# Where the gated cross-attention mixes a batch, when it asks for the transposed scores, and which step holds which projection product

## The chip, the core and the metric

The kernel runs on one core of a Trainium2 chip. The core has a matrix engine (PE, with its own weight loads, PEld), a vector engine (DVE), a scalar engine (ACT), a general engine (POOL) and a sequencer that issues DMAs (SP); 16 DMA engines serve the core. Each engine works through its own list of instructions in order and waits on semaphores for the others. The metric is the device time of one execution in microseconds (us), here the median of several.

## The reference, cut to what matters

Sixteen batches of 128 tokens with 512 features pass through a decoder layer (self-attention, cross-attention to `ctx_2048`, an MLP) and then through a gated cross-attention. All three attentions have 16 heads of 32 features. All is float32. The part that the change touches is the attention itself:

```
def attention(q, k, v, mask):
    scores = jnp.einsum('bhqd,bhkd->bhqk', q, k) / jnp.sqrt(jnp.float32(HD))
    scores = scores * mask - 10000.0 * (1.0 - mask)
    probs = jax.nn.softmax(scores, axis=-1)
    return jnp.einsum('bhqk,bhkd->bhqd', probs, v)
...
Q = (hidden_states @ Wq.T)...
K = (a @ Wk.T)...
V = (a @ Wv.T)...
attn = jax.nn.softmax(scores, axis=-1)
out = jnp.einsum('bhts,bhsd->bhtd', attn, V)
return hidden_states + jnp.tanh(gate) * out
```

The first function is the decoder's (used twice), the lines after the dots are the gated attention's.

## The kernel before

**Stages.** The program has three stages. The decoder's two attentions come first, then the MLP, then the gated attention. Tile names end in the attention's letter: A is self-attention, B the decoder's cross-attention, D the gated attention. The sixteen batches are worked in four groups ("sections") of four; the decoder has eight sections (A0 to A3, then B0 to B3), the gated attention four (D0 to D3).

**Units and steps.** `attend` (called once for the decoder with `ready` false, once for the gated attention with `ready` true) runs over steps numbered `k`. A batch takes four steps and its scores (`sc`, four banks of PSUM) are made on PE at the step with `k % 4 == 0`. A unit is four heads of one batch; each step adds one unit. Unit `u` is masked and its least value found on DVE around step `u` (`scale_unit`; the list `SCALED` puts the first unit of a batch in its first step, the second and third in the next, the fourth in the one after), exponentiated on ACT at step `u + 1` (`exp_unit`), normalised on DVE (a reciprocal) and POOL at `u + 2` (`norm_unit`), and turned on DVE and sent to DRAM (`away`) by SP at `u + 3` (`turn_unit`). Two units are fetched back in another order as one pair into a `pT` tile by four DMAs on SP (`receive_pair`). `pT` has three buffers and the `s` tile of a unit seven. The last four units of the gated attention are turned on PE instead (`turn_by_array`, `tp`).

**Mixing.** `mix` multiplies the weights of one batch, its two pairs, with the values `v` on PE (`av`). ACT then copies the result out (`mT`). Two steps later the result is projected by PE (`mo`), or, in the first three gated groups, put away for a later projection. The dictionaries `mixed_at` and `received_at` (line 702 on) hold in which step batch `b` is mixed and in which two steps its pairs are asked for. In a decoder step that makes scores the mixing stands at the head of the step, before the scores; the gated run mixes later in the step, after the step's jobs, and copies out at the start of the next step.

**What else a step does.** In the order of the code: asking for pairs, the work left over from the step before (`due`: DVE sums first, then ACT copies), the step's jobs, the projection of an earlier batch, the preparation of a later section (`prepare`: loads, transposes, copies into `T` tiles by ACT), turning, exponentials and normalisation, masking. While one section's attention runs, the jobs make the next section's queries, keys and values. Each of these three is a product cut into seven quarter-size products (Strassen's scheme, `block_product`), eight matmuls of 256 columns each, numbered 1 to 7. Products 1, 6 and 7 share the bank `mm0` and are copied out by ACT; 5 and 3 share `mm1`, 2 and 4 take `pt` banks, and DVE adds these up. The sums of inputs that the products need come from POOL. `GATED_BLOCKS` (line 508) says which of the 16 steps of a section holds which of the seven products of queries, keys and values. While the last section D3 runs, the output projections of the first three groups take their place (`deferred_jobs`).

**Order.** The engines keep the program's order (`InOrder`), so the step and the place in it fix the order on each engine and in SP's queue. Nearly every instruction goes through the recording helper at line 51, so the profile's rows all carry L51 and are told apart by tile.

```
SCALED = ((0,), (1, 2), (3,), ())
...
if ready and b * GB == last:
    k = last + 7
else:
    for half in range(2):
        received_at.setdefault(at + 2 * half, []).append(b * GB + 2 * half + 1)
mixed_at[k] = b
...
beside_scores = done is not None and m == 0
```

With `GB` = 4, unit number `b * GB + 1` stands for the first pair of batch `b`, `b * GB + 3` for the second. `last` is the first unit of the last batch.

Of the kernel before, what the change touches and what calls it, by code (L numbers as in the profile page):

```python
# [26 lines left out]
GB = 4  # L27
# [27 lines left out]
def decoder_then_gated_cross_attention(ctx: ExitStack, tc: tile.TileContext, a: dict, out: bass.AP):  # L55
# [24 lines left out]
    def afterwards(engine, do):  # L80
        late[engine].append(do)

    def due():

        left = [do for queue in (late["dve"], late["act"]) for do in queue]
        for queue in late.values():
            queue.clear()
        for do in left:
            do()
# [396 lines left out]
    def by_quarters(t):  # L486
# [20 lines left out]
    FIRST_CROSS_BLOCKS = {6: (1,), 7: (2, 6), 8: (5,), 9: (7, 4), 11: (3,)}, CROSS_BLOCKS[1]  # L507
    GATED_BLOCKS = (
        {0: (1,), 1: (2, 6), 2: (5, 7), 3: (4,), 5: (3,)},
        {5: (1,), 6: (2, 6), 7: (7,), 8: (5,), 9: (4,), 10: (3,)},  # L510
        {11: (1, 2), 12: (6,), 13: (5, 7), 14: (4,), 15: (3,)},
    )
    DEFERRED_BLOCKS = (
        {0: (1,), 1: (2, 6), 2: (5, 7), 3: (4,), 5: (3,)},
# [31 lines left out]
    def scores(bt):  # L546
        sec, t = bt.sec, slice(bt.b * S, (bt.b + 1) * S)
        for j in range(GB):
            bt.sc[j] = ps("sc", f"sc_{bt.name}_{j}")
        for c in range(KC):  # L550
            for j in range(GB):
                r = slice(j * HD, (j + 1) * HD)
                nc.tensor.matmul(
                    bt.sc[j][:, c * S : (c + 1) * S], sec.q[r, c, t], sec.k[r, c, t], start=True, stop=True
                )
# [4 lines left out]
    def by_head(t):  # L560
        return t.rearrange("p n c j -> p c n j")
# [59 lines left out]
    def receive_pair(bt, j):  # L621

        pT = work.tile([P, NQ, 2, KC, Q], F32, tag="pT", name=f"pT_{bt.name}_{j}", bufs=3)
        for m in range(NQ):
            nc.sync.dma_start(
                out=pT[m * Q : (m + 1) * Q].rearrange("k n u c q -> k n (u c q)"),
                in_=bt.away[j // 2][m].rearrange("(n k) u x -> k n (u x)", k=Q),
            )
        for u in range(2):
            bt.pT[j - 1 + u] = pT[:, :, u]  # L630

    def mix(bt):
        sec, b = bt.sec, bt.b
        av = ps(mixed_in[0], f"av_{bt.name}")
        for c in range(KC):
            for j in range(GB):
                h = c * GB + j
                nc.tensor.matmul(
                    av[j * HD : (j + 1) * HD, c * S : (c + 1) * S], sec.v[:, b, h * HD : (h + 1) * HD],
                    bt.pT[j][:, :, c, :], start=True, stop=True,  # L640
                )
        at_end = work.tile([P, KC, S], F32, tag="s", name=f"mT_{bt.name}", bufs=7) if bt.by_array else None
        mT = bt.mT = sec.mixed_tile(b) if at_end is None else at_end

        def mixed_out():
            if sec.v_bias is None:
                nc.scalar.copy(mT, av.rearrange("p (c q) -> p c q", q=S))
            else:
                for c in range(KC):
                    nc.scalar.activation(  # L650
                        mT[:, c], av[:, c * S : (c + 1) * S], AF.Identity, bias=col(sec.v_bias[0], sec.v_bias[1] + c)
                    )

        return mixed_out

    def out_project_last(bt):

        for n in range(2):
            at_ = slice(n * HF, (n + 1) * HF)
            mm = ps("mm", f"mo_{bt.name}_{n}")  # L660
            for c in range(KC):
                nc.tensor.matmul(
                    mm[:, 0:HF], bt.mT[:, c, :], bt.sec.w_o[:, c, at_], start=(c == 0), stop=(c == KC - 1)
                )
            bt.sec.finish(mm[:, 0:HF], bt.b, at_)

    def out_project(bt):
        mm = ps(mixed_in[0], f"mo_{bt.name}")
        for c in range(KC):
            nc.tensor.matmul(mm, bt.mT[:, c, :], bt.sec.w_o[:, c, :], start=(c == 0), stop=(c == KC - 1))  # L670
        afterwards("dve", lambda: bt.sec.finish(mm, bt.b))
# [13 lines left out]
    def attend(sections, ready, others, after=None):  # L685

        if not ready:
            sections[0].start(sections[1])
        units, batches = [], []
        projected = deque()

        last = (len(sections) * GB - 1) * GB

        def by_transfer(n):

            return min(n, last) if ready else n  # L700

        mixed_at, received_at = {}, {}
        for b in range(len(sections) * GB):
            k, at = (b + 3) * GB, (b + 2) * GB
            sooner = 2 if ready else min(2, max(0, b + 4 - len(sections) * GB))
            k, at = k - sooner, at - sooner
            if ready and b * GB == last:
                k = last + 7
            else:
# [4 lines that stand above are left out]
        def step(k, bt=None, jobs=(), ahead=None):  # L714

            m = k % GB
            mixed_in[0] = "sc" if not ready and k > last + 2 else "mm"
            pairs, done = received_at.get(k, []), mixed_at.get(k)
            beside_scores = done is not None and m == 0
            if beside_scores:  # L720
                mixed_out = mix(batches[done])
            if m == 0 and bt is not None:
                scores(bt)
            for pair in pairs:
                receive_pair(*units[pair])
            due()
            if beside_scores:
                mixed_out()
                projected.append((k, batches[done]))
            for job in jobs:  # L730
                job()
            last_mix = ready and k == last + 7
            if last_mix:
                afterwards("act", mix(batches[-1]))
                projected.append((k, batches[-1]))
            if projected and k - projected[0][0] >= (1 if ready and bt is None else 2):
                before = projected.popleft()[1]
                if before.by_array:
                    out_project_last(before)
                elif before.sec.deferred:  # L740
                    afterwards("act", lambda: before.sec.put_away(before))
                else:
                    out_project(before)
            first_turned = ready and k == last + 6
            if first_turned:
                turn_by_array(*units[k - 3])
            if done is not None and not (beside_scores or last_mix):
                mixed_out = mix(batches[done])
                if ready:
                    afterwards("act", mixed_out)  # L750
                else:
                    mixed_out()
                projected.append((k, batches[done]))
            if ahead is not None:
                ahead.prepare(k % NS)
            if 0 <= k - 3 < len(units) and not first_turned:
                (turn_unit if k - 3 < by_transfer(k) else turn_by_array)(*units[k - 3])
            def norm():
                if 0 <= k - 2 < len(units):
                    norm_unit(*units[k - 2])  # L760

            def exp():
                if 0 <= k - 1 < len(units):
                    least_unit(*units[k - 1])
                    exp_unit(*units[k - 1])


            for do in (exp, norm) if ready else (norm, exp):
                do()
            if bt is not None:  # L770
                for j in SCALED[m]:
                    scale_unit(bt, j)
                if bt.b < sec.by_head_from:
                    bt.sec.add_mask(by_head(bt.s[m]), bt.b)

        k = 0
        for i, sec in enumerate(sections):
            jobs = others() if i + 1 == len(sections) else sections[i + 1].jobs()
            ahead = sections[i + 2] if i + 2 < len(sections) else after if i + 2 == len(sections) else None
            for b in range(GB):  # L780
                bt = Batch(sec, b)
                batches.append(bt)
                for m in range(GB):
                    units.append((bt, m))
                    step(k, bt, jobs.get(k % NS, ()), ahead)
                    k += 1
        while projected or k < len(units) + 2 * GB:
            step(k, jobs=jobs.get(k - len(units) + NS, ()))
            k += 1
# [1038 lines left out]
```

## Time and profile before

| what | value |
|---|---|
| median of 3 runs | 1159.51 us (1159.28 to 1161.2) |
| the profiled execution's own time | 1162.35 us |
| its span, first to last instruction | 1160.6 us |
| PE busy in it | 1132.9 us |
| decoder, first to last mixing on PE | 84.3 to 553.2 us |
| gated attention, first scores to end | 946.1 to 1160.6 us |
| DMA traffic, mean over the span | 224 GB/s |

The profile comes from one execution with the hardware profiler on. Its span is what the views below are drawn on; the time of that same execution stands 1.75 us above its span, and 2.84 us above the median of the unprofiled runs. A row of the timeline gives the start, the duration, the engine, the tiles written and read and how many instructions were merged in it; in square brackets stands how long the engine had been idle and what ended the wait. SPq rows are DMAs being issued; the landing comes later. Matmul ends are modelled, so rows of PE overlap by about 0.1 us.

### The profile page before, as it was taken

What the parts mean: (1) busy time and instruction counts of PE and PEld (TensorE: products, weight loads), DVE (VectorE), ACT (ScalarE), POOL (GpSimd) and SP (SyncE); (2) the same over time, 40 slices, a digit from 0 to 9 for tenths busy, and PEclk for the clock granted to TensorE, in tenths of its full rate; (3) what the DMA queues carried; (4) which work ended last, traced back from release to release, by engine and by line L of the source; (5) the groups of instructions that cost most, each with busy time, mean ns of one, the idle gap of its engine ahead of it and who ended that gap; (6) DMA issues with size and microseconds to landing.
All of it is one profiled execution on the core that took longest, in us unless ns stands there. A gap on an engine that the chain in (4) does not pass through costs nothing.

```text
span 1160.6 us, 22182 instructions
## 1 busy us (share of the span) xinstructions
PE 1132.9 (98%) x7246; PEld 875.1 (75%) x7246; DVE 742.9 (64%) x1919; ACT 612.0 (53%) x2142; POOL 694.4 (60%) x633
## 2 busy tenths in 40 slices
PE   9999999999999999989899999999999999999998
PEld 8877777666666757446688888888888877878875
DVE  6678978798787786866554634443342247767754
ACT  3567676767767766663231233223222237867663
POOL 6798888788868675752333514443342168545883
PEclk9999999999999999989999999999999999999999
DMA  6688878999889889997787696697447827987975
GB/s 220 162 206 227 228 208 212 280 232 255 209 221 222 218 231 254 297 272 247 236 260 238 189 280 192 200 283 254 154 154 234 258 51 200 249 236 222 272 216 175
DMA packets 325285, 259.81 MB, mean 224 GB/s; under 512 B 83561, under 2 KB 280625, under 8 KB 320305
## 3 DMA queue, kind: packets, MB, share of 16 engines
q1 hardware_dynamic: 325128, 258.38, 78.1%
q8 instruction: 58, 0.95, 0.4%
q14 instruction: 59, 0.48, 0.1%
q10 hardware_dynamic: 40, 0.01, 0.0%
HBM read 163.94 MB, written 94.37 MB: 223 GB/s over the span
## 4 chain that ended last, share of the span: by engine, by line
PE 45%; DMA 6%; POOL 2%; DVE 2%; SPq 1%; ACT 1%; issue 1%; DVEq 0%; ACTq 0%; POOLq 0%
PE o L51 16%; PE h L51 15%; PE mm_v_D L51 4%; PE mm_q_D L51 3%; PE mm_o_D L51 1%; DMA back_x<-turned_x 1%; DMA pT_D<-away_D 1%; PE mm_k_D L51 1%; DMA pT_B<-away_B 1%; SPq L51 1%; PE av_D L51 1%; DMA away_D<-s_D 1%; PE mo_D L51 1%; DMA away_B<-s_B 1%; PE sc_D L51 1%
## 5 line engine op out<-in xcount | busy, mean ns | idle before, releaser
L51 DVE TENSOR_TENSOR h<-h,h 128x512 f32<-128x512 f32 x80 | 54.9, 686 | 113.9 <-PE h L51 113.9
L51 ACT ACTIVATE h<-h 128x512 f32<-128x512 f32 x64 | 40.3, 630 | 162.3 <-DVE h L51 162.3
L51 ACT ACTIVATE s_A<-s_A,mn_A 128x128 f32<-128x128 f32 x256 | 99.4, 391 | 45.7 <-issue 23.8
L51 ACT ACTIVATE s_B<-s_B,mn_B 128x128 f32<-128x128 f32 x256 | 99.4, 392 | 29.7 <-issue 14.0
L51 POOL TENSOR_TENSOR s_D<-s_D,sum_D 128x512 f32<-128x512 f32 x64 | 66.5, 1040 | 59.9 <-DVE sum_D L51 53.1
L51 POOL TENSOR_TENSOR s_B<-s_B,sum_B 128x512 f32<-128x512 f32 x64 | 66.8, 1044 | 56.4 <-DVE sum_B L51 47.8
L51 ACT ACTIVATE s_D<-s_D,mn_D 128x128 f32<-128x128 f32 x256 | 99.1, 392 | 0.4 <-issue 0.4
L51 POOL TENSOR_TENSOR s_A<-s_A,sum_A 128x512 f32<-128x512 f32 x64 | 66.5, 1039 | 31.0 <-DVE sum_A L51 25.3
L51 POOL TENSOR_TENSOR s_A<-s_A,ma 128x512 f32<-128x512 f32 x64 | 81.8, 1279 | 5.1 <-DVE s_A L51 4.1
L51 POOL TENSOR_TENSOR s_B<-s_B,mask 128x512 f32<-128x512 f32 x60 | 76.4, 1273 | 2.4 <-DVE s_B L51 1.5
L51 POOL TENSOR_TENSOR rstd_aD<-rstd_aD,mhalf 128x1 f32<-128x1 f32 x12 | 6.6, 549 | 114.8 <-DVE rstd_aD L51 101.6
L51 POOL TENSOR_TENSOR sh<-h 128x512 f32<-128x512 f32 x32 | 40.7, 1272 | 50.8 <-ACT h L51 49.9
L51 PE MATMUL h<-sx,t 128*128 128x256 f32 x256 | 60.6, 379 | 2.0 <-ACT h L51 2.0
L51 PE MATMUL h<-T_C,w 128*128 128x256 f32 x256 | 61.2, 382 | 1.3 <-DVE h L51 1.3
L51 PE MATMUL h<-T_C,t 128*128 128x256 f32 x256 | 60.6, 379 | 1.0 <-DVE h L51 1.0
L51 PE MATMUL o<-t,h 128*128 128x256 f32 x256 | 60.5, 379 | 0.0
L51 PE MATMUL o<-w,h 128*128 128x256 f32 x256 | 60.5, 379 | 0.0
L51 PE MATMUL o<-t,sh 128*128 128x256 f32 x256 | 60.5, 379 | 0.0
L51 DVE CUSTOM_DVE_ANT_0 s_D<-sc_D,gmask 128x128 f32<-128x128 f32 x256 | 57.1, 283 | 1.0 <-DMA turned_x<-x_D 0.9
L51 PE MATMUL mo_A<-w_ao,mT_A 128*128 128x512 f32 x128 | 57.5, 592 | 0.0
L51 PE MATMUL mo_B<-w_co,mT_B 128*128 128x512 f32 x128 | 57.5, 592 | 0.0
L51 PE MATMUL mm_q_B<-T_B,w_cq 128*128 128x512 f32 x128 | 57.4, 596 | 0.0
(335 smaller groups left out, 3007.4 us busy)
## 6 DMA issues: line engine op xcount, KB each, us to landing
t<-kept SPq DMA_DIRECT2D x24, 1024.0 KB, 8.3
away_A<-s_A SPq DMA_DIRECT2D x64, 256.0 KB, 3.3
pT_A<-away_A SPq DMA_DIRECT2D x128, 128.0 KB, 3.8
away_B<-s_B SPq DMA_DIRECT2D x64, 256.0 KB, 3.3
pT_B<-away_B SPq DMA_DIRECT2D x128, 128.0 KB, 4.8
away_D<-s_D SPq DMA_DIRECT2D x60, 256.0 KB, 3.4
pT_D<-away_D SPq DMA_DIRECT2D x120, 128.0 KB, 2.8
w<-in_L_xattn_w_dram SPq DMA_DIRECT2D x24, 512.0 KB, 5.5
```

Source lines behind the costliest of these rows:

```text
L51: return lambda *args, **kw: self.tc.keep_in_program_order(call(*args, **kw))
```

## The change

The change touches two places.

```
     GATED_BLOCKS = (
         {0: (1,), 1: (2, 6), 2: (5, 7), 3: (4,), 5: (3,)},
-        {5: (1,), 6: (2, 6), 7: (7,), 8: (5,), 9: (4,), 10: (3,)},
-        {11: (1, 2), 12: (6,), 13: (5, 7), 14: (4,), 15: (3,)},
+        {4: (1,), 5: (2,), 6: (6,), 7: (5, 7), 9: (4, 3)},
+        {9: (1,), 10: (2, 6), 11: (5,), 12: (7,), 13: (4,), 15: (3,)},
     )
...
         for b in range(len(sections) * GB):
-            k, at = (b + 3) * GB, (b + 2) * GB
-            sooner = 2 if ready else min(2, max(0, b + 4 - len(sections) * GB))
-            k, at = k - sooner, at - sooner
+            sooner = min(2, max(0, b + 4 - len(sections) * GB))
+            k, at = (b + 3) * GB - sooner, (b + 2) * GB - max(1, sooner)
```

In steps, for batch `b` (the last three batches of a run have their own numbers, by `sooner`):

| run | pairs asked for, before | after | mixed, before | after |
|---|---|---|---|---|
| decoder, batches 0 to 28 | 4b+8, 4b+10 | 4b+7, 4b+9 | 4b+12, head | 4b+12, head |
| decoder, batches 29 to 31 | unchanged | | unchanged | |
| gated, batches 0 to 12 | 4b+6, 4b+8 | 4b+7, 4b+9 | 4b+10, after the jobs | 4b+12, head |
| gated, batch 13 | 4b+6, 4b+8 | 4b+7, 4b+9 | 62 | 63, after the jobs |
| gated, batches 14, 15 | unchanged | | unchanged | |

So the gated run's mixing moves two steps later, to the head of a step with the next-but-two batch's scores, and its result is copied out by ACT within that step instead of at the start of the next one. The projection or putting away that follows two steps after a mixing moves with it. The products of the next section's keys and values move to the steps shown; the queries' stay. No instruction is added or taken away on any engine, and POOL's list is the same, instruction by instruction.

Between two scores of the gated run PE now finds these products of the next section (q, k, v with the number of the product), in the order of its list:

| steps of a section | before | after |
|---|---|---|
| 0 to 3 | q1 q2 q6 q5 q7, mixing, q4 | q1 q2 q6 q5 q7 q4, mixing |
| 4 to 7 | q3 k1 k2 k6, mixing, k7 | k1 q3 k2 k6 k5 k7, mixing |
| 8 to 11 | k5 k4 k3, mixing, v1 v2 | k4 k3 v1 v2 v6 v5, mixing |
| 12 to 15 | v6 v5 v7 v4, mixing, v3 | v7 v4 v3, mixing |

The mixing at the end of each "after" row is the one at the head of the following step, just ahead of its scores.

## The prediction

> **What bounds the kernel now.** I read the page's busy times first, then the list of waits of PE, then PE's timeline around the long waits, then the other engines there.
>
> ```profile
> PE 1132.9 (98%) x7246; PEld 875.1 (75%) x7246; DVE 742.9 (64%) x1919; ACT 612.0 (53%) x2142; POOL 694.4 (60%) x633
> ```
>
> PE is idle for 1160.6 - 1132.9 = 27.7 us. The change adds and removes no instruction, so it can win only from those 27.7 us and from what a lowered matrix clock costs inside the busy time. The waits say which part is in reach:
>
> ```profile
> PE av_B L51 <- DMA pT_B<-away_B: 6.7, 2, 5.5
> PE av_D L51 <- DMA pT_D<-away_D: 3.0, 3, 2.3
> ...
> PE sc_D L51 <- DVE mn_D L51: 0.9, 1, 0.9
> ...
> PE mm_k_D L51 <- ACT k_D L51: 0.7, 1, 0.7
> ```
>
> The columns are sum, count and longest. The first two rows are mixings (`av`) whose pair had not landed. The largest one, in section B3, is at step 124:
>
> ```profile
> 504.13 0.41 PE L51 MATMUL av_B<-pT_B,v_B 128*32 128x128 f32 x4
> 510.09 1.92 PE L51 MATMUL av_B<-pT_B,v_B 128*32 128x128 f32 x28 [5.54 <-DMA pT_B<-away_B]
> 511.94 2.09 PE L51 MATMUL sc_B<-k_B,q_B 32*128 32x128 f32 x32
> 513.96 4.71 PE L51 MATMUL mm_v_D<-w_gv,T_a 128*128 128x512 f32 x8
> 518.51 3.60 PE L51 MATMUL mo_B<-w_co,mT_B 128*128 128x512 f32 x8
> ```
>
> Four matmuls on the first pair run, the other 28 wait for the second. After the wait the same work is slower: 1.92 us where 28 such matmuls take 1.07 elsewhere, 2.09 where scores take 1.17, 4.71 where eight matmuls of 512 columns take 3.60. That is 0.85 + 0.92 + 1.11 = 2.9 us more, and the granted clock from 508 to 514 us is 0.60. So this wait costs 5.5 + 2.9 = 8.4 us. The gated attention has a smaller copy of it in D1, and the rows after it show a stretch that I need below:
>
> ```profile
> 1024.33 0.41 PE L51 MATMUL av_D<-pT_D,v_D 128*32 128x128 f32 x4
> 1027.05 1.07 PE L51 MATMUL av_D<-pT_D,v_D 128*32 128x128 f32 x28 [2.31 <-DMA pT_D<-away_D]
> 1028.05 5.38 PE L51 MATMUL mm_v_D<-w_gv,T_a 128*128 128x256 f32 x16
> 1033.36 1.17 PE L51 MATMUL sc_D<-k_D,q_D 32*128 32x128 f32 x32
> 1034.46 1.99 PE L51 MATMUL mm_v_D<-gsums,gsums_a 128*128 128x256 f32 x8
> 1036.29 1.89 PE L51 MATMUL mm_v_D<-w_gv,gsums_a 128*128 128x256 f32 x8
> 1038.02 1.89 PE L51 MATMUL mm_v_D<-gsums,T_a 128*128 128x256 f32 x8
> ...
> 1044.50 1.17 PE L51 MATMUL sc_D<-k_D,q_D 32*128 32x128 f32 x32
> ```
>
> Sixteen such matmuls take 3.72 us elsewhere, here 5.38: 1.7 us of clock (granted 0.72 from 1026 to 1032). This wait costs 2.3 + 1.7 = 4.0 us.
>
> **The change, part by part.** *Asking one step sooner in the decoder.* The late pair is asked for at step 122; it moves to the head of step 121, just behind the send of step 120.
>
> ```profile
> 498.33 0.38 SPq L51 DMA_DIRECT2D away_B<-s_B  x1
> 499.16 0.34 SPq L51 DMA_DIRECT2D kept_v_D<-v_D  x1
> ...
> 502.23 1.95 SPq L51 DMA_DIRECT2D pT_B<-away_B  x4
> ```
>
> Its four issues would start at 498.8 instead of 502.2, 3.4 us sooner. Its inputs are away since 491.3 and its buffer was freed by the mixing that ended at 496.0, so nothing holds it. What it is moved past on SP is one `kept_v_D` store, two `back_C` loads, one weight load and the send of unit 118. They start 2 us later. The loads feed the MLP, which starts at 526 us, the store the gated attention; the send's pair is asked for at 511.65. Now its landing:
>
> ```profile
> 503.88 6.12 DMA pT_B<-away_B
> ```
>
> This row of the chain of waits says that the last of the four, issued at 503.88, landed after 6.12 us. At the same price the new one lands at 510.0 - 3.4 = 506.6. PE is there at 504.5, so 2.1 us of the 5.5 stay: 3.4 gained. The other decoder wait, 1.1 us at 465, is shorter than a step and goes; if SP moves up with PE the gain there carries over whole, if not it lengthens the rest of the big wait. I take half, 0.6. For the clock I have 2.9 now, and afterwards a gap of 2.1 to 3.2 us, near the 2.31 that cost 1.7; gaps of 1.12, 1.73 and 1.96 us elsewhere left the clock at 1.00. Half of 1.7 gives a gain of 2.9 - 0.8 = 2.1. Sum 3.4 + 0.6 + 2.1 = 6.1. The next to be late would be the mixing at 525.5. Its pair stays where it is, issued from 511.65; with 1.65 between first and last issue and a median landing of 5.4 us (transfers into `pT_B`, 440 to 560 us) it is there at 518.7, and PE would come at 519.4. It just fits. Bounds: nothing (the pair lands when the busy DMA engines let it) and 6.7 + 2.9 = 9.6.
>
> The Trainium skill, page "DMA: Bandwidth & Descriptors", section on the anatomy of one DMA (on GpSimd's path), puts a transfer at about 2 us plus its bytes by 436 GB/s, which makes an estimated 2.3 us for 128 KB; the 6.12 us above were measured with the DMA engines busy throughout (share 1.06 from 508 to 514). By the page the pair would land at 502.8, the wait would vanish and the decoder would gain 9.6; the row decides.
>
> *Mixing two steps later, asked for one step later, in the gated run.* A pair gets three steps from its last send to the request instead of two, and three to its mixing. SP waited 42.9 us in 29 places for `away_D` to land before it could ask. I count all three `av_D` waits but the one at the end (0.4, on the unchanged batches) as gone: 0.32 + 2.31, and 1.7 of clock. Bounds 0 and 4.3; what hides the landing now is two steps of products.
>
> *Products in other steps.* k7 no longer follows k6 at once, so the 0.68 wait for ACT's copy in D0 goes; k5 now stands ahead of the scores that waited 0.92 there, so these meet finished masks. Gain 1.6, bounds 0 and 1.6. But the 21 products of a section, 6+5+5+5 between the scores, become 6+6+6+3. In the last quarter PE has two products less to do while DVE still needs the same chain: the last mask of a batch stands behind the reciprocal of its first unit, that behind the unit's exponentials, those behind ACT's copies. In D1:
>
> ```profile
> 1036.49 0.59 ACT L51 COPY v_D<-mm_v_D 128x512 f32<-128x512 f32 x1 [2.63 <-PE mm_v_D L51]
> 1036.97 0.82 ACT L51 ACTIVATE T_a<-back_a,vcols 128x512 f32<-128x512 f32 x1
> ...
> 1039.94 0.59 ACT L51 COPY v_D<-mm_v_D 128x512 f32<-128x512 f32 x1 [0.62 <-PE mm_v_D L51]
> 1040.43 0.82 ACT L51 ACTIVATE T_a<-back_a,vcols 128x512 f32<-128x512 f32 x1
> ```
>
> The first copy is of v6, the second of v7, and the chain ends with the last mask at 1043.86. After the change v7 has v6's place and the second copy is gone: ACT is free at 1039.24 and saves 1.2 us to 1040.43. The mask ends at 1042.7. PE saves v6 and v5, 1038.02 - 1034.46 = 3.6, and wants to start the scores at 1044.50 - 3.56 = 1040.9. A new wait of 1.7 us at `sc_D`. The same reading of D0 (mask ends at 993.23, ACT saves 1.2, scores at 993.26 - 3.56) gives 2.3; in D2, where DVE is held by POOL's normalisation, 1089.45 - 1.05 against 1090.80 - 3.56 gives 1.1. D3 keeps its products. Sum 5.1, and half of 1.7 for the clock after the 2.3 us gap: 5.9. Queued behind are only PE's next products; they wait with it. Bounds: 0 if ACT runs ahead, and, if the masks end no sooner than now (9.9, 9.3 and 8.6 us after the scores, for 6.4 us of PE's work), 3.5 + 2.9 + 2.2 = 8.6 plus 3 x 1.7 = 13.7.
>
> The Trainium skill, page "TensorE: Matmul & The Clock Gate", section on HAM oscillation, lets PE idle for up to about 3.4 us before the clock drops; the row at 1028.05 shows a drop after 2.31. By the page neither of my two half-charges of 0.8 would fall due, and the sum would be 1.6 us better.
>
> *The tail.* Batch 12 is projected two steps later, batch 13's copy comes behind one more unit's exponentials (1.55 us), and products 5 and 7 come 3.5 us sooner. The waits there hang on POOL, whose list is unchanged. I take 0, bounds -1 and +1.
>
> **Sum.** -6.1 - 4.3 - 1.6 + 5.9 + 0 = -6.1 us. The profiled execution would come to 1162.35 - 6.1 = 1156.2, its span to 1154.5; on the median, 1159.51 - 6.1 = 1153.4.
>
> **Rivals.** *The short quarter decides* (slower). If the masks end no sooner than now, the gated run pays 13.7 for 5.9; with a decoder gain of 6.1 that is 1161.2. It turns slower once the three waits and their clock exceed 12.0 us, from 2.3 us each on with 1.7 of clock each. For it: D0 and D1 had 0.03 and 0.6 us to spare now. Against: 1.2 us of the chain is a copy that goes. *The DMA engines set the landing, not the order.* The decoder keeps its 5.5 and gains 0.6 at most: 1159.51 - 0.6 = 1158.9. For it: a DMA share above 1. Against: one store and three loads of 256 KB each stand behind the pair instead of ahead. *All waits go*: 9.6 in the decoder, 5.9 in the gated run, and 2 us of new waits: 1146.0. For it: ACT idles 2.63 us ahead of its copy. That the mixing doesn't reach the scores can't be: PE's list has it there.
>
> **Chances.** Forecast 55% (its own range 1149 to 1157), short quarter 13%, DMA 14%, all gone 18%. The range 1146.0 to 1159.5 leaves out most of the first rival and the far end of the last. A measurement tells no change from one within 0.2%, 1157.2 to 1161.8. Forecast and "all gone", with some of the DMA case, make faster 78%; most of the DMA case and half the short quarter make the same 14%; slower 8%.
>
> **What would show it.** Right: no 5.5 us before the `av_B` of step 124 and at most 3 left; no `av_D` waits in D0 and D1; three `sc_D` waits on DVE of 1 to 2.5 us at the scores that open D1, D2 and D3; granted clock near 1.00 from 1020 on. Wrong: the decoder's wait unchanged, `sc_D` waits above 2.3 us with a lowered clock behind them, or new waits of a product for POOL's sums in D0.

## The result, and the profile after

The changed kernel takes 1168.18 us (median of 6 runs, 1166.97 to 1171.61). The kernel before took 1160.36 us beside it (6 runs, 1159.23 to 1162.71). The ratio is 1.0063, with a 95% interval of 1.0047 to 1.0080: the change makes the kernel slower.

The two traces split this in two parts that point opposite ways:

| stretch of the span | before | after |
|---|---|---|
| start of the span to the first scores of the gated attention | 946.1 us | 940.9 us |
| first scores of the gated attention to the end | 214.5 us | 226.4 us |
| whole span | 1160.6 us | 1167.3 us |

The decoder gives 5.2 us. The gated attention costs 11.9. The busy times of the page after hide both: PE is busy for half a microsecond more than before.

```profile
PE 1133.4 (97%) x7246; PEld 878.2 (75%) x7246; DVE 744.7 (64%) x1919; ACT 611.3 (52%) x2142; POOL 694.7 (60%) x633
```

The list of PE's waits after (sum, count, longest, in us; dots stand for rows left out) shows what is in place of the old waits.

```profile
PE av_D L51 <- DMA pT_D<-away_D: 7.9, 3, 5.8
PE av_B L51 <- DMA pT_B<-away_B: 3.2, 2, 1.9
PE mm_q_D L51 <- ACT q_D L51: 2.2, 1, 2.2
...
PE mm_k_D L51 <- DVE q_D L51: 1.8, 1, 1.8
...
PE av_D L51 <- DVE x L51: 1.5, 1, 1.5
...
PE sc_D L51 <- DVE mn_D L51: 1.4, 1, 1.4
...
PE mo_D L51 <- DVE x L51: 0.5, 1, 0.5
```

The decoder's row went from 6.7 to 3.2. The gated mixings' row, which the change was to empty, went from 3.0 to 7.9, and a product now waits for ACT and one for DVE. Row by row the gated stretch waits 4.9 (av_D for transfers) + 2.2 (mm_q) + 1.8 - 0.7 (mm_k) + 0.5 (sc) + 0.3 (tail: 1.5 + 0.5 - 1.7) = 9.0 us more. In the view by stretches PE's busy time there grew from 204.94 to 207.58 us for the same 1753 matmuls, 2.6 us more. Together 11.6 of the 11.9. The 2.6 is a balance of two things. The rows that ran on a lowered clock (granted 0.51 to 0.53) are some 6.1 us longer than the same rows at full speed, against 1.7 us before. The other way, the gated runs without a drop of the clock show the same matmuls shorter when the mixing stands right ahead of scores: 200.7 to 202.5 us in runs 2, 6, 8, 9 and 10 below, against 203.45 in run 3 and 203.60 in run 1.

**The largest wait.** PE's timeline after, at the opening of D3 (start, duration, tiles, count; the wait in brackets):

```profile
1082.12 1.99 PE L51 MATMUL mm_v_D<-gsums,T_a 128*128 128x256 f32 x8
1083.95 1.89 PE L51 MATMUL mm_v_D<-w_gv,gmask 128*128 128x256 f32 x8
1085.67 1.89 PE L51 MATMUL mm_v_D<-gsums,T_a 128*128 128x256 f32 x8
1087.49 0.41 PE L51 MATMUL av_D<-pT_D,v_D 128*32 128x128 f32 x4
1093.69 1.92 PE L51 MATMUL av_D<-pT_D,v_D 128*32 128x128 f32 x28 [5.78 <-DMA pT_D<-away_D]
1095.54 2.09 PE L51 MATMUL sc_D<-k_D,q_D 32*128 32x128 f32 x32
```

After three products PE is at the mixing, and the second pair is missing. The waiting matmuls and the scores then run at about half the clock (1.92 us where 1.07 is usual, 2.09 for 1.17; granted 0.51 from 1092.6 to 1099.6 us). Why the pair was late is in SP's timeline of the same stretch, where each row is an issue:

```profile
1077.56 1.92 SPq L51 DMA_DIRECT2D pT_D<-away_D  x4
1079.52 0.52 SPq L51 DMA_DIRECT2D kept_mT_D<-mT_D  x1
1084.54 0.82 SPq L51 DMA_DIRECT2D mixed<-kept_mT_D  x2
1085.47 0.92 SPq L51 DMA_DIRECT2D away_D<-s_D  x2
1086.48 2.23 SPq L51 DMA_DIRECT2D pT_D<-away_D  x4
```

Between the second row and the third SP does nothing for 4.5 us. The second row stores batch 7's mixed rows in DRAM; the third fetches the same rows back for the deferred projection. SP's own list of waits for 1076 to 1096 us names it:

```profile
SPq L51 <- DMA kept_mT_D<-mT_D: 4.4, 1, 4.4
```

Sends and the pair request stand behind the fetch. For about the last 2 us of this wait, and until the fetch moves its first data, the DMA engines have next to nothing to do: in their busy share from 1070 to 1100 us, in 40 slices of 0.75 us, the zeros are 1082.75 to 1085.

```profile
DMA  9589999999999999600018499999999999999999
```

The last issue, at 1088.24, landed 5.32 us later (chain of waits), at 1093.55.

**The wait of a product for ACT.** ACT's timeline after, in D1:

```profile
992.05 0.18 ACT L51 ACTIVATION_READ_ACCUMULATOR s_D<-s_D,mn_D 128x1 f32 x1
994.88 0.58 ACT L51 COPY mT_D<-av_D 128x512 f32<-128x512 f32 x1 [2.65 <-DMA kept_mT_D<-mT_D]
995.37 0.59 ACT L51 COPY q_D<-mm_q_D 128x512 f32<-128x512 f32 x1
```

and PE's behind it:

```profile
990.15 3.72 PE L51 MATMUL mm_q_D<-T_D,w_gq 128*128 128x256 f32 x16
996.10 2.80 PE L51 MATMUL mm_q_D<-x,gsums 128*128 128x256 f32 x8 [2.23 <-ACT q_D L51]
```

There is one `mT` tile (`bufs=1`). ACT may copy the next batch's mixed rows into it only when the store of the last ones has landed. ACT waits 2.65 us for that; the copy of product q1 stands behind, and q6 needs q1's bank. Over the gated run, the tile's view counts ACT's waits of this kind as 3.3 us in one place before, and after as

```profile
  DMA kept_mT_D<-mT_D: 10.8, 6
```

Both waits so lead to the same instruction, the store of the mixed rows, which the prediction had not priced. Before, it was issued at the head of step 4b+13, and the next copy into the tile came at the head of 4b+15. The change moves the store with the mixing to the head of 4b+15, behind that step's pair request, and the next copy to within step 4b+16. A step is about 3 us.

### The profile page after: what moved, and what is told of

Same layout as the page of the kernel before. It is cut to its first block, busy times and chain, and to the rows that moved or that the text cites. A ratio compares the mean times of both kernels' runs of the same rounds, so it can differ in the third digit from the quotient of the medians.

```text
span 1167.3 us, 22179 instructions
## 1 busy us (share of the span) xinstructions
PE 1133.4 (97%) x7246; PEld 878.2 (75%) x7246; DVE 744.7 (64%) x1919; ACT 611.3 (52%) x2142; POOL 694.7 (60%) x633
```

## The experiments

All times are medians; each ratio is against the kernel before on the same chip, with its 95% interval. A difference of two ratios is given in points of 0.01, and is uncertain by some 0.2 to 0.3 points. A trace shows one execution: the decoder is the same in the changed kernel and in runs 1 to 11, yet its waits for pairs add up to anything from 1.9 to 3.8 us there, so a difference of 2 us between two traces says little by itself.

**1. The decoder's part alone.** Against the changed kernel (old `GATED_BLOCKS` too, so that the gated run is that of before):

```
-            sooner = min(2, max(0, b + 4 - len(sections) * GB))
+            sooner = 2 if ready else min(2, max(0, b + 4 - len(sections) * GB))
```

> Only the decoder's requests are moved one step sooner; the gated run and its products stay as before. Theory (the decoder part gains, the gated part loses): the gated scores start about 5 us sooner than before (946.1 us there, 940.9 after), the gated stretch keeps its 214 us, so the time is 5 us under the kernel before, ratio about 0.9955. Rival (the sooner start is paid back later, because the gated stage hangs on something that does not start sooner): the gated stretch grows by the same 5 us and the ratio is 1.000.

Measured: 1155.27 us, 0.9953 (0.9933 to 0.9973). PE's waits in it:

```profile
PE av_D L51 <- DMA pT_D<-away_D: 2.9, 3, 1.8
PE av_B L51 <- DMA pT_B<-away_B: 2.3, 2, 1.4
...
PE tp_D L51 <- POOL s_D L51: 1.7, 1, 1.7
...
PE sc_D L51 <- DVE mn_D L51: 0.9, 1, 0.9
...
PE mm_k_D L51 <- ACT k_D L51: 0.7, 1, 0.7
```

Of these rows only the decoder's differs from before by more than 0.1, 2.3 for 6.7. The decoder part is worth about 0.47%, and all that is lost is lost in the gated run.

**2. The changed kernel with the old products**, so with mixing at the head and later requests, but no short quarter. Edit: the old `GATED_BLOCKS`.

> The changed kernel with the key and value products of the gated run back in their old steps (6, 5, 5, 5 products between scores instead of 6, 6, 6, 3). Theory (the quarter with three products is what costs): the waits at the first scores of D1, D2 and D3 shrink to at most 3 us in all, the wait of k5 for the query sum in D0 (1.8 us) goes; time 1154 to 1158 us, ratio about 0.997. Rival (the mixing at the head costs by itself, because ACT must copy within the step and the store of the mixed tile comes later): it stays near the changed kernel, ratio 1.004 or more.

Measured: 1162.43 us, 1.0009 (0.9989 to 1.0029). Both the expected range and the rival's (1.004 or more) missed it: the old products take 0.54 points off, half of the 1.10 that the changed kernel stands above run 1, and the mixing with its requests keeps 0.56. The short quarter is not the whole cost. Without it ACT waits for the store even more, 15.8 us in seven places; products wait for ACT's copies (1.40, 0.90, 0.68, 0.90 and 0.77 us; the 0.68 was there before) and a pair is 2.64 us late at 1090.9 us, behind a wait of 4.1 us of SP between store and fetch.

**3. The new products without the new mixing.** Edit: the line of run 1 in the changed kernel, with its new `GATED_BLOCKS`.

> The gated run asks and mixes as before, the products stand in the new steps, the decoder's requests are the new ones. Theory (three products are too few to cover the chains whichever step mixes): new waits in the last quarter of D0, D1 and D2, 1 to 3 us each with their clock, so the time is 1158 to 1164 us. Rival (the new steps are harmless by themselves): as the decoder part alone, ratio about 0.9955.

Measured: 1157.8 us, 0.9983 (0.9964 to 1.0002), just under the expected range and 0.30 points above run 1, with intervals that overlap. Its waits in the gated run:

```profile
PE sc_D L51 <- DVE mn_D L51: 3.5, 3, 1.3
...
PE mm_k_D L51 <- DVE q_D L51: 1.8, 1, 1.8
```

The three waits for masks are there (1.00, 1.22 and 1.26 us), 3.5 us in all for the 5.1 that the prediction had, and no clock drop follows them; the second row is one that was not forecast.

**4. The changed kernel with the last fetches of mixed rows later.**

```
-  [7, 7, 9, 9, 11, 11, 13, 13]),
+  [7, 7, 9, 9, 13, 13, 14, 14]),
```

> The changed kernel with the fetches of the second group's mixed tokens at steps 13, 13, 14, 14 instead of 11, 11, 13, 13 of D2, so that SP does not meet them right behind the store that they read. Theory (SP's wait of 4.5 us there makes the pair of the mixing at 1087 us late): the wait of 5.8 us and its clock (2.7 us) shrink to 1.5 us or less, time 6 us under the changed kernel, about 1162. Rival (the pair is late anyway because only three products stand between its request and its mixing): less than 2 us are gained.

Measured: 1162.63 us, 1.0009 (0.9994 to 1.0024), 0.54 points less than the changed kernel. The wait at the opening of D3 fell from 5.78 to 0.39 us:

```profile
1089.06 1.07 PE L51 MATMUL av_D<-pT_D,v_D 128*32 128x128 f32 x28 [0.39 <-DMA pT_D<-away_D]
```

In this trace the pair's request starts 3.5 us after the store instead of 7.0. SP's stop between store and fetch was the cause of the late pair, though not of its whole length: with five products of cover (run 2) much the same stop leaves 2.64 us. ACT's waits for the store stayed (10.3 us in six places).

**5 and 6. The store one step sooner**, in the changed kernel (5) and in run 2 (6):

```
-            if projected and k - projected[0][0] >= (1 if ready and bt is None else 2):
+            if projected and k - projected[0][0] >= (1 if ready and (bt is None or projected[0][1].sec.deferred) else 2):
```

> The changed kernel with one condition other: a gated batch's mixed rows are put away one step after the mixing instead of two, so the store is issued at the head of step 4b+14 instead of 4b+15, two steps ahead of the next copy into the same single mT tile. Theory (the store stands too close ahead of the next copy and of SP's fetch): ScalarE's waits on the store before its mT copy fall from 10.8 us in all to under 4, the 2.23 us wait of q6 behind ScalarE's late q1 copy goes with the clock loss behind it (1.8), and SP's 4.5 us wait between the store of batch 7 and its fetch falls under 2.5, so that the 5.78 us wait at the opener of D3 falls under 2 with its clock loss (2.7): 1157 to 1161 us against 1168. Rival (the late copies come from the copy standing within its own step, and the 5.78 us is the transfer's own landing): 1165 to 1169 us, waits as they are.

> Mixing at the head of a step and the requests of the change, the products of the kernel before, and the store of the mixed rows one step sooner as in the run beside it. Theory: what the head mixing costs against the decoder part alone (1162.4 against 1155.3 us) is the store close to the next copy; with the store sooner the waits of products on ScalarE's copies (1.40, 0.90, 0.68, 0.90, 0.77 us) and the 2.64 us on the last transfers go: 1154 to 1158 us. Rival (the copy and the mixing at the head of the step cost by their own place): 1160 to 1163 us.

Measured: 1159.82 us, 0.9975 (0.9952 to 0.9997) for 5, and 1155.61 us, 0.9947 (0.9929 to 0.9964) for 6. Moving the stores by one step takes 0.88 points off the changed kernel and 0.62 off run 2. In 5, ACT waits nowhere for the store and q6 not at all; 2.45 us are left at the opening of D3, a little more than expected, where PE still comes after three products and SP waits 1.4 us for the store. In 6, three waits of keys' products for ACT stay (2.4 us in all), and SP's timeline before the opening of D3 reads

```profile
1069.34 0.52 SPq L51 DMA_DIRECT2D kept_mT_D<-mT_D  x1
1071.63 0.38 SPq L51 DMA_DIRECT2D away_D<-s_D  x1
1072.11 1.95 SPq L51 DMA_DIRECT2D pT_D<-away_D  x4
1074.16 0.84 SPq L51 DMA_DIRECT2D mixed<-kept_mT_D  x2
1075.10 2.02 SPq L51 DMA_DIRECT2D away_D<-s_D  x2
1077.21 1.97 SPq L51 DMA_DIRECT2D pT_D<-away_D  x4
```

Store and fetch are 4.8 us apart, with a request between them, and SP stands still for neither. PE then goes through without a wait:

```profile
1082.90 1.89 PE L51 MATMUL mm_v_D<-gsums,T_a 128*128 128x256 f32 x8
1084.72 1.08 PE L51 MATMUL av_D<-pT_D,v_D 128*32 128x128 f32 x32
1085.73 1.17 PE L51 MATMUL sc_D<-k_D,q_D 32*128 32x128 f32 x32
```

**7. Run 2 with the copy at the head of the next step**, which puts the store two steps ahead of the next copy without moving the store:

```
             if beside_scores:
-                mixed_out()
+                if ready:
+                    afterwards("act", mixed_out)
+                else:
+                    mixed_out()
```

> Mixing at the head of a step and the requests of the change, the products of the kernel before, the store at its place in the changed kernel, but the copy of the mixed rows out of its bank is put to the head of the next step, as it was before the change (store at the head of 4b+15, next copy at the head of 4b+17). Theory (store close to copy): the distance is two steps again, ScalarE's waits on the store go, 1155 to 1159 us; the 2.64 us wait on the last transfers stays, since SP still waits for the store ahead of its fetch. If only the copy's place within its step counts the same falls here but not in the run with the sooner store. Rival (neither counts; the mixing itself is in the way): 1161 to 1164 us.

Measured: 1159.73 us, 0.9982 (0.9966 to 0.9997), just above the expected range. ACT's waits for the store fell from 15.8 to 4.4 us (one place), as the distance says. But keys' products now wait 5.0 us for ACT in four places, and 2.03 us remain at D3's opening, behind a wait of 3.9 us of SP for the store.

**8. Run 2 with the later fetches of run 4.**

> Head mixing and requests of the change, the old products, the store at its place in the changed kernel, and the last four fetches of mixed rows in steps 13, 13, 14, 14 of their section instead of 11, 11, 13, 13. With the store one step sooner the same kernel fell from 1162.4 to 1155.6 us. If ScalarE's copies behind the store carry that cost, the waits of products on ScalarE (1.40, 0.90, 0.68, 0.90, 0.77 us) stay and only the 2.64 us wait on the last transfers goes: 1159 to 1161 us. Rival (SP's wait between store and fetch carries all of it): 1155 to 1157 us.

Measured: 1159.59 us, 0.9991 (0.9975 to 1.0006). No pair is late at D3's opening, and ACT still waits 16.6 us in seven places. It stands 0.18 points below run 2 and 0.44 above run 6, so with the old products the fetch would carry the smaller part of what the store's place costs and ACT's copies the larger; the intervals of runs 2 and 8 overlap, so the split itself is rough. With the new products it is the other way about: run 4 gave 0.54 of the 0.88 points of run 5.

**9 and 10. The decoder's part with the gated mixing one step later** (4b+11, after the jobs; requests as before), without and with the sooner store:

```
             k, at = (b + 3) * GB - sooner, (b + 2) * GB - max(1, sooner)
+            if ready and b < len(sections) * GB - 2:
+                k += 1
```

> The decoder part alone (1155.3 us), with the gated mixing one step later (step 4b+11 instead of 4b+10) and no other request, copy or store moved against it. Its transfers then have a step of 11 to 13 us more. The two waits on them in the decoder part alone (0.84 at 1007.4 us and 1.82 at 1019.0 us, 2.66 us in all) go: 1152 to 1154.5 us. Rival (step 4b+11 holds products whose copies stand in the way, as in the head mixing): 1155 to 1159 us.

> The gated mixing one step later than before (4b+11), and the store one step sooner, with the decoder part. The run with the mixing one step later alone had ScalarE waiting 9.9 us in six times for the store, and products behind its copies (1.02, 0.77, 0.74 us). With the store two steps ahead again these copies start on time and the 1.02 and 0.74 us go: 1152.5 to 1155 us, at or below both kernels and the decoder part alone. Rival (the copies are late for another reason): 1154.5 to 1157 us.

Measured: 1155.07 us, 0.9938 (0.9918 to 0.9959) for 9, and 1151.58 us, 0.9921 (0.9905 to 0.9937) for 10. Run 9 stands just above its expected range, at the lower edge of the rival's. (A step is about 3 us; the 11 to 13 us in its expectation are a batch's four steps.) The two waits on transfers are gone, but ACT waits 9.9 us in six places for the store. By the code the store stands two steps ahead of the copy there, as it did before; but it now shares its step with a pair request, and SP issues it 7.5 us after the copy (median) where run 10 has 4.3. With the sooner store, by the code three steps ahead of the copy and not the two that were expected, ACT's waits are gone. Run 10 has the lowest time of all, below its expected range, in a gated stretch of 210.4 us without a drop of the clock:

```profile
PE mm_k_D L51 <- ACT k_D L51: 3.2, 3, 1.7
...
PE sc_D L51 <- DVE mn_D L51: 0.9, 1, 0.9
PE av_D L51 <- DMA pT_D<-away_D: 0.8, 1, 0.8
```

The 0.8 is in the tail; no other gated mixing waits. Run 10 is faster than both kernels; its interval still touches that of run 1.

**11. The decoder's part with the sooner store** (edit of runs 5 and 6 in run 1).

> The decoder part alone with the store one step sooner (three steps ahead of the next copy of the mixed rows instead of two). With two steps ScalarE waited for the store once, 3.1 us, and no product waited for it. If two steps are enough: 1154 to 1157 us, the waits on the transfers at 1007.4 and 1019.0 us (0.84 and 1.82 us) as they were. Rival (SP's queue gains from the sooner store too): these two fall and it is 1151 to 1154 us.

Measured: 1158.28 us, 0.9977 (0.9961 to 0.9993). Above the range, with an interval that overlaps run 1's. ACT's one wait for the store (3.1 us) is gone, but the gated mixings wait 4.0 us for transfers instead of 2.9, one of them 2.38 with a drop of the clock. Where two steps of distance were already there, a third gives nothing; whether it costs is open.

**12. The kernel before with the store one step later**, nothing of the change in it:

```
-            if projected and k - projected[0][0] >= (1 if ready and bt is None else 2):
+            if projected and k - projected[0][0] >= (1 if ready and bt is None else 3 if projected[0][1].sec.deferred else 2):
```

> The kernel before, with one condition other: the gated rows are put away three steps after their mixing instead of two, so the store stands at the head of step 4b+14, behind that step's pair request, and the next copy into the one mT tile at the head of 4b+15. Nothing of the changed kernel is in it. Theory (a store one step ahead of the next copy costs by itself): ScalarE's waits on the store rise from 3.3 us to 9 to 16 us, products wait for ScalarE's late copies, and it is 4 to 8 us slower than before, 1164.5 to 1169 us. Rival (it costs only together with mixing at the head): 1160 to 1163 us.

Measured: 1165.83 us, 1.0040 (1.0024 to 1.0056), 5.1 us above the kernel before beside it (1160.71). ACT's timeline has the same row as the changed kernel's, and PE's the same victim:

```profile
999.77 0.59 ACT L51 COPY mT_D<-av_D 128x512 f32<-128x512 f32 x1 [3.18 <-DMA kept_mT_D<-mT_D]
```

```profile
1003.21 2.99 PE L51 MATMUL mm_q_D<-x,gsums 128*128 128x256 f32 x8 [2.87 <-ACT q_D L51]
```

In the traces the gated stretch is 219.8 us for the 214.5 before. SP waits 4.0 us between store and fetch here too, and a pair is 2.37 us late at 1094.6 us, so both of the routes seen in the changed kernel are in these 5 us. So the place of the store costs by itself, in a kernel whose mixing and products did not move. The runs side by side, with the median time from a store's issue to the start of the next copy into the tile, from the traces (seven of the eight stores; the copy after the last goes to another tile):

| kernel | store to next copy | ACT's waits for the store | ratio |
|---|---|---|---|
| before | 5.8 us | 3.3 us, 1 | 1 |
| before, store later (12) | 3.4 | 9.7, 4 | 1.0040 |
| changed | 3.3 | 10.8, 6 | 1.0063 |
| changed, store sooner (5) | 7.6 | none | 0.9975 |
| old products (2) | 4.1 | 15.8, 7 | 1.0009 |
| old products, store sooner (6) | 8.1 | 2.2, 1 | 0.9947 |
| mixing at 4b+11 (9) | 4.2 | 9.9, 6 | 0.9938 |
| mixing at 4b+11, store sooner (10) | 7.0 | none | 0.9921 |

Landings of these stores, where the trace has them, took 2.9 to 4.1 us. A copy that waits starts when its store has landed, so 3.3 to 4.2 us in the first column is mostly the landing itself; where the median is 5.8 us or more, ACT waited once or not at all. Three of the four pairs differ by 0.40 to 0.88 points; the fourth, 0.17, is within its intervals, though its waits show the same. A second `mT` tile, which would take the dependency away, was not tried.

## Why the prediction was wrong, by its own steps

**The decoder, -6.1: right.** The trace after has the first gated scores 5.2 us sooner, and run 1 measured 0.47%, some 5.5 us. At step 124 the rows are

```profile
503.48 1.07 PE L51 MATMUL av_B<-pT_B,v_B 128*32 128x128 f32 x28 [1.35 <-DMA pT_B<-away_B]
504.48 1.17 PE L51 MATMUL sc_B<-k_B,q_B 32*128 32x128 f32 x32
```

1.35 us for the 2.1 forecast, and full speed behind it. One detail was wrong: the next mixing, of which I wrote "It just fits", waited 1.87 us.

**Mixing later in the gated run, -4.3: this is the step that failed.** I counted "all three `av_D` waits but the one at the end (0.4, on the unchanged batches) as gone", and held that "what hides the landing now is two steps of products". The waits were 7.9 us after. Beside the same products the move of the mixing costs 0.56 points (runs 1 and 2) or 0.80 (run 3 and the changed kernel), some 6.5 and 9.3 us, where I forecast a gain of 4.3. The part on the requests held: SP's waits for `away_D` between 940 and 1110 us fell from 38.7 us to 2.5. What I left out is that the step moves more than the mixing. The copy and the store of the mixed rows move with it, the store lands in another place of SP's queue, and the distance to the next copy into the one tile shrinks from two steps to one (in the traces from 5.8 us to 3.3). I had described that move and gave it no price. Runs 2 and 6 give it 0.62 points with the old products, run 5 and the changed kernel 0.88: the larger part of the 1.10 points between run 1 and the changed kernel, the new products having the rest. With the store in a good place (run 6) the new mixing has a gated stretch of 212.0 us against 213.0 in run 1, two single executions: a gain is not shown even then, and the ratios cannot tell it from none.

The page "DMA: Bandwidth & Descriptors" of the Trainium skill (section on the anatomy of one DMA) says that a transfer's wait is served on the sequencer that issues it, before it is handed over. SP's 4.4 us agree: a fetch that waited for a store held up sends and a request that had nothing to do with it, while the DMA engines, for about its last 2 us, stood near zero.

**Products in other steps, -1.6: right as far as it went.** The 0.68 and the 0.92 are gone. But k5 shares the bank `mm1` with q3, and q3's sum is DVE's. Right after k2 and k6, k5 came before DVE had added it, and waited 1.81 us (1.8 in runs 3, 4 and 5 too, none in runs 1, 2 and 6):

```profile
962.61 1.99 PE L51 MATMUL mm_k_D<-gsums_a,w_gk 128*128 128x256 f32 x8 [1.81 <-DVE q_D L51]
```

I had moved k5 and looked only at the scores behind it, not at the bank ahead of it.

**The short quarter, +5.9: right mechanism, too large.** The term was 5.1 of waits and 0.8 of clock; run 3 has 3.5 and none. In the changed kernel only 1.4 shows as waits for masks; at D1 and D3 the mixing just ahead of the scores waits 1.72 and 5.78 us, and the scores then find their masks done. What I missed is that three products also leave the transfers of that mixing less cover: run 5 waits 2.45 us at D3's opening, where run 6 with five products waits for nothing.

**The tail, 0: right.** `tp` no longer waits 1.7, and 1.5 and 0.5 came in its place.

Of the rivals none named the store. The slower one had the right sign, but its mechanism is the smaller part: the new products cost 0.28 points (runs 5 and 6) to 0.54 (run 2 and the changed kernel). Its time, 1161.2, was 7 us short.

## What to carry to other kernels

When a step is moved, list what is chained to it, and follow each chain through the next reuse of its buffer: a tile with one buffer has a store that must land before the next copy, and the distance between the two is part of the schedule. In an in-order queue an instruction's place in the code is not when it is issued; a transfer that has to wait delays what stands behind it (here a fetch right behind its store held the queue for 4.5 us), and a store behind a pair request is itself issued later (here 7.5 us after its copy instead of 4.3). Where work is taken from one place, look at all that it covered, transfers and bank reuse as well as the wait that was in view.

## What the runs showed of the hardware

The matrix clock fell after less idle time than the prediction had counted on, which had seen gaps of up to 1.96 us leave it alone. Three stretches of the trace after, with the columns start and end, length, busy time and count of PE, PEld, DVE, ACT and POOL, then the granted clock, DMA share and GB/s:

```profile
997.00:1000.60 3.60, 3.60 (x10) 2.86 (x10) 3.08 (x19) 2.15 (x12) 2.27 (x2) 0.53 0.97 233
1041.40:1045.00 3.60, 3.57 (x30) 3.10 (x31) 2.81 (x12) 2.59 (x11) 2.72 (x4) 0.53 0.96 272
1092.60:1099.60 7.00, 5.91 (x65) 4.97 (x66) 3.32 (x14) 0.58 (x1) 5.29 (x5) 0.51 1.10 308
```

They follow waits of 2.23 us, of 0.43 and 1.38 close together, and of 5.78. Run 5 dropped after a wait of 1.57 with one of 0.19 shortly ahead of it, run 7 after 2.03; waits of 1.81 (run 3), 1.75 (run 10) and even 2.64 us (run 2, at 1090.9 us) left the clock alone. So between 1.5 and 2.7 us both happen, and two short waits can do what one long one does. The page "TensorE: Matmul & The Clock Gate" of the Trainium skill (section on HAM oscillation) puts the limit at gaps of some 3.4 us; the rows show drops at about half of that, and not every time.
